# Layer 2's grouped attention: queries and keys of sequences 1 to 7 turned by VectorE blocks and DMA instead of TensorE transposes

## The chip, the cores and the metric

The kernel runs on one core of one Trainium2 chip. The metric is the device time of one execution in microseconds (us). Before the change it is 2081.69 us, the median of three runs (2081.62 to 2082.62). The core has a matrix engine (TensorE, PE in the profile, with its weight loads in the row PEld), a vector engine (VectorE, DVE), an activation engine (ScalarE, ACT), a general engine (GpSimd, POOL), and SyncE (SP), which here issues every DMA. Each engine works through its own list of instructions in order and waits on semaphores for the others. Everything is fp32.

## The reference, cut to what matters

The model has four layers over an input of 8 sequences x 256 tokens x 512 features. Layers 0 and 1 are attention with an MLP, layer 2 is attention alone, and layer 3 is a set of expert MLPs. The change touches layer 2:

```python
def _L2_cond_ref(x, t_emb, W_ada, b_ada, Wq, Wkd, Wku, Wvu, Wo):
    ...                                  # h: layer norm of x, scaled and shifted per sequence
    q = (h @ Wq.T).reshape(B, T, 16, 32).transpose(0, 2, 1, 3)
    c_kv = h @ Wkd.T                     # latent of 128
    k = (c_kv @ Wku.T).reshape(B, T, 4, 32).transpose(0, 2, 1, 3)
    v = (c_kv @ Wvu.T).reshape(B, T, 4, 32).transpose(0, 2, 1, 3)
    q = q * cos + _rotate_half(q) * sin
    k = k * cos + _rotate_half(k) * sin
    ...                                  # each key head serves four query heads
    scores = jnp.einsum('bhtd,bhsd->bhts', q, k_exp) / jnp.sqrt(32)
    scores = jnp.where(mask[None, None], -jnp.inf, scores)
    attn = jax.nn.softmax(scores, axis=-1)
    y = jnp.einsum('bhts,bhsd->bhtd', attn, v_exp)
    return x + y.transpose(0, 2, 1, 3).reshape(B, T, C) @ Wo.T
```

## The kernel before, in words

A token tile is 128 tokens on the 128 partitions, so a sequence is two tiles (`TB`). Products contract over partitions. Projected queries and keys come out with tokens on partitions, but the scores need features on partitions, so both have to be turned by 90 degrees.

**The attention loop.** `attend` (L655) runs the 8 sequences, each with 4 groups of 4 heads. For each group `scored` (L685) issues the score products into four PSUM banks (tag A), and `softmax` (L706) does, head by head, a biased minimum on VectorE (L743) and an exponential with a running sum on ScalarE (L747). Then the weights have to be turned as well. In layer 2, for heads 0 and 1 of each group of the first seven sequences, VectorE transposes 32 x 32 blocks (L752), and five DMAs per group carry the blocks through DRAM (four out in `put`, L545, and one back, L756). For heads 2 and 3 TensorE does three 128 x 128 transposes per head (`turned`, L783), and VectorE or ScalarE copies the result out of PSUM. `weighted` (L808) forms the context, two groups late; `divided` (L830) multiplies by the reciprocal sums.

**The work between the groups.** The rest is dealt into the loop from `self.queue`. `some(us)` (L208) adds a credit and draws generators, each of which yields what its products cost by the author's estimate. It is called three times per group. Two generators matter: `added` (L1310), the output product of the sequence before (eight 128x512 products), and `project2` (L1666), the projection of the next sequence. The projection has the latent (four products of 256 columns), per tile the query product (four of 512 columns), the rotation by `rope` (L649 and L650 on VectorE, then one add on POOL, L1683 for the queries and L1688 for the keys), and the key and value product (L1685). Its input `hT` was normed, turned by VectorE (L534) and sent through DRAM one sequence earlier (`prepare`, `put`, `fetch`; eight DMAs back, L567), and is scaled and shifted at the end of a sequence (L490, L491).

**Queries and keys turned.** `queries_turned` (L1255) makes, per tile, four TensorE transposes of the queries (L1258) into a PSUM bank and one of the keys (L1264), and copies the two banks out, one on VectorE and one on ScalarE (L480, L481, L483, L484). That is ten transposes and four copies per sequence.

**What sets the order.** The program's order is not the order of an engine's list. A scheduler draws instructions at build time, by their priority and by its own estimate of when their inputs are ready, so that work later in the program can be put ahead of an instruction that it expects to wait. `keep_in_program_order` pins chosen instructions. On the chip each list is then worked through strictly in order.

Of the kernel before, what the change touches and what calls it, by code (L numbers as in the profile page):

```python
# [34 lines left out]
P = 128  # L35
# [53 lines left out]
ROUND = 1.5 * 2.0**23  # L89
PI_BELOW = 3.1415925  # L90


# [87 lines left out]
class Program:  # L180
    def __init__(self, ctx, tc, d, out):
        self.ctx, self.tc, self.nc, self.d, self.out = ctx, tc, tc.nc, d, out
        self.n = 0
        self.queue, self.credit = [], 0.0
        self.ready, self.calls = {}, 0
# [22 lines left out]
    def some(self, us):  # L208


        self.credit += us
        self.calls += 1
        while self.credit > 0 and self.queue:
            try:
                did = next(self.queue[0])
            except StopIteration:
                self.queue.pop(0)
                continue
            if did is not None:
                self.credit -= did  # L220
            elif us < 1e6:
                break

    def rest(self):
        self.calls += 100
        self.some(1e9)
        self.credit = 0.0

    def setup(self):
# [39 lines left out]
        self.turns = [self.tc.dram_tile([P, KC * S], F32, name=f"turn{i}") for i in range(3)]  # L271
        self.n_turn = 0
        self.flips = [self.tc.dram_tile([P, 8 * P], F32, name=f"flip{i}") for i in range(4)]
        self.n_flip = 0
# [270 lines left out]
    def put(self, kept, tile):  # L545

        to = kept.rearrange("(c i) (a x) -> a i c x", c=4, a=4)
        for a in range(4):
            self.nc.sync.dma_start(
                to[a], tile[32 * a : 32 * a + 32, :].rearrange("p (c x) -> p c x", c=4)  # L550
            )

    def fetch(self, calls):

        for (name, b), entry in self.ready.items():
            hT, _, kept, _, _ = entry
            if kept is None:
                continue
            entry[2:4] = None, self.calls + calls
            if self.stage(name)[5]:  # L560
                self.nc.sync.dma_start(hT, kept)
                continue
            parts = kept.rearrange("p (a k t j) -> p k t a j", a=4, k=KC, t=TB)
            to = hT.rearrange("p (k t a j) -> p k t a j", k=KC, t=TB, a=4)
            for k in range(KC):
                for t in range(TB):
                    self.nc.sync.dma_start(to[:, k, t], parts[:, k, t])  # L567
# [87 lines left out]
    def attend(self, name, n_groups, hd, project, value, finish, work, key_tiles=(2, 2), biased=None,  # L655
               extra=None, then=None, spare=None, inverse=None, after=None, rooms=None, contexts=None):

# [27 lines left out]
        def scored(b, g):  # L685
# [3 lines left out]
            for j0 in range(0, 4, rows):  # L689
                for q in range(TB):  # L690
                    for j in range(j0, j0 + rows):
                        lhsT, rhs = lhs_rhs[j]
                        keys = rhs(wide[q])
                        if j < self.in_blocks(name, b):

                            keys = keys.rearrange("p (k c i) -> p c k i", c=4, i=32)
                        mm = nc.tensor.matmul(  # L697
# [122 lines left out]
        def divided(b, o, by):  # L820
            for c in range(nch):
                chunks = ctx.setdefault(b, [])
                if b == late:
                    out = spare()[len(chunks)]
                elif contexts is not None:
                    out = contexts[:, b % 2 * 4 + len(chunks), :]
                else:
                    out = self.t([P, S], "ctxT")
# [9 lines left out]
        for i in range(B * n_groups + 1):  # L838
# [59 lines left out]
            else:  # L898
# [5 lines left out]
                while due and due[0][0] <= i:  # L904
                    _, b, g, (pT, by) = due.pop(0)
                    divided(b, weighted(b, g, pT), by)
                    if g == n_groups - 1:
                        if b != late:
                            self.queue.insert(0, outcome(b))
                        got.pop(b)  # L910
# [356 lines left out]
    def project0(self, b, got):  # L1267
# [32 lines left out]
        def scores(g, j):  # L1300
# [3 lines left out]
                lambda q: qT[rows, c, q * P : (q + 1) * P],  # L1304
                lambda n: kT[rows, 0:n],
            )
# [151 lines left out]
    def project1(self, b, got):  # L1458
# [69 lines left out]
        def scores(g, j):  # L1528
            rows = slice(32 * j, 32 * j + 32)
            return (  # L1530
                lambda q: qT[rows, g, q * P : (q + 1) * P],
                lambda n: kT[rows, g, 0:n],
            )
# [132 lines left out]
    def project2(self, b, got):  # L1666
# [3 lines left out]
        qT = self.t([P, KC, S], "qT")  # L1670
        kT, v = self.keys_values(b, ((S,), (TB, P)))
        m = self.bank("C")[:, :S]
        yield from self.product_steps(m, lambda k: w[:, k, 512:640], lambda k: hT[:, k, :])
        cT = self.bank("n")[:, :S]
        nc.scalar.copy(cT, m)
        turn = []
        for t in range(TB):
            cs, sn = self.rope2[:, t, 0, 0, :], [self.rope2[:, t, 1, s, :] for s in range(2)]
            tok = slice(t * P, (t + 1) * P)
            q = self.bank("C")  # L1680
            yield from self.product_steps(q, lambda k: hT[:, k, tok], lambda k: w[:, k, 0:512])
            qr, qb = self.rope(self.bank("qk"), q, cs, sn, 16, 16)
            nc.gpsimd.tensor_tensor(qr, qr, qb, ALU.add)  # L1683
            kv = self.bank("C")[:, :S]
            nc.tensor.matmul(kv, cT[:, tok], w[:, 0, 640:896], start=True, stop=True)  # L1685
            kr, kb = self.rope(self.t([P, P], "kr", 2), kv[:, :P], cs, sn, 4, 16)
            nc.vector.tensor_copy(v[:, t, :], kv[:, P:])
            nc.gpsimd.tensor_tensor(kr, kr, kb, ALU.add)  # L1688
            turn.append((t, qr, kr))
            yield 0.43  # L1690
        for t, qr, kr in turn:
            yield None
            self.queries_turned(t, qT, kT, qr, kr, 1.0 / math.sqrt(32.0))
            yield 0.53

        def scores(g, j):
            rows = slice(32 * j, 32 * j + 32)
            return (
                lambda q: qT[rows, g, q * P : (q + 1) * P],
                lambda n: kT[rows, 0:n],  # L1700
            )
# [4 lines left out]
    def layer2(self):  # L1706
# [10 lines left out]
            inverse=[spare[:, i, :] for i in range(4, 8)],  # L1717
            rooms=self.rooms, contexts=contexts,
        )
# [280 lines left out]
```

## Time and profile before

| what | value |
|---|---|
| median of three runs | 2081.69 us |
| the profiled execution's own time, and its span | 2078.34 us, 2076.6 us |
| PE busy over the span | 2006.0 us (97%) |
| DVE, ACT, POOL busy | 1365.2, 748.1, 334.0 us |
| mean granted TensorE clock | 0.987 |
| layer 2's loop: first score product of sequence 0 to that of sequence 7 | 1668.22 to 1893.51 us |
| mean ns of one: query transpose (L1258), POOL add of the queries (L1683) in the loop | 311, 1333 |

A row of the view by stretches gives the stretch, the busy time of PE, PEld, DVE, ACT and POOL in it with the number of instructions, then the granted TensorE clock (1.00 is full), the mean busy share of the 16 DMA engines and GB/s. In the timeline of an engine a row gives the start, the time to the end of the last of its instructions, the engine, the line, the operation with output and inputs, and in brackets the idle time before it with what ended it. Matmuls overlap, so the time that one costs is the distance from its start to the next start, not its duration.

### The profile page before, as it was taken

How to read it: one execution, taken by the hardware profiler on the slowest of the kernel's cores; microseconds unless marked ns; L12 is line 12 of the kernel's file. 1: busy time of each engine (PE TensorE's matmuls, PEld its weight loads, DVE VectorE, ACT ScalarE, POOL GpSimd, SP SyncE). 2: the span in 40 equal slices, each digit the busy share in tenths (PEclk: the TensorE clock that was granted, in tenths of full speed). 3: DMA queues.
4: the chain of work that ended last, by engine and by line, in shares of the span. 5: the costliest groups of instructions: out<-in, count | busy, mean ns of one | idle time of the engine just before them, and what ended most of it. 6: DMA issues, size and time to landing. Idle time of an engine off the chain costs nothing.

```text
span 2076.6 us, 36333 instructions
## 1 busy us (share of the span) xinstructions
PE 2006.0 (97%) x12818; PEld 1480.9 (71%) x12818; DVE 1365.2 (66%) x4429; ACT 748.1 (36%) x2332; POOL 334.0 (16%) x372
## 2 busy tenths in 40 slices
PE   7999999999999999999999999999999989989999
PEld 4555579999999999954544447999999854445454
DVE  6867766656675555656676766776765678776544
ACT  4333421111111111136565653222222256565644
POOL 1111200000000000054544531000000021101411
PEclk9999999999999999999999999999999989999999
DMA  8543361112130010334555543233211245653411
GB/s 306 166 119 90 102 215 48 65 42 64 61 110 26 17 31 16 96 99 129 131 143 141 141 123 115 89 101 116 87 60 48 67 113 137 158 145 97 126 40 42
DMA packets 223685, 208.91 MB, mean 101 GB/s; under 512 B 83536, under 2 KB 184976, under 8 KB 223120
## 3 DMA queue, kind: packets, MB, share of 16 engines
q1 hardware_dynamic: 223504, 206.59, 34.3%
q8 instruction: 102, 1.67, 0.3%
q14 instruction: 79, 0.65, 0.1%
HBM read 135.46 MB, written 71.07 MB: 99 GB/s over the span
## 4 chain that ended last, share of the span: by engine, by line
PE 78%; DVE 7%; ACT 7%; DMA 4%; issue 2%; POOL 2%; SPq 1%; DVEq 0%; ACTq 0%; POOLq 0%
PE C L1024 29%; PE A L1073 18%; PE C L631 17%; PE A L697 3%; ACT p L747 3%; PE C L808 3%; ACT wbig L747 2%; PE C L783 2%; PE C L1887 2%; PE A L1789 1%; DMA turn<-hT 1%; PE C L1822 1%; DVE st L449 1%; DMA wbig<-in_wgT 1%; DVE n L650 1%
## 5 line engine op out<-in xcount | busy, mean ns | idle before, releaser
L1024 PE MATMUL C<-hT,wbig 128*128 128x128 f32 x3072 | 416.4, 275 | 0.0
L1024 PEld LDWEIGHTS C<-hT,wbig 128*128 128x128 f32 x3072 | 388.8, 192 | 9.0 <-issue 2.4
L631 PE MATMUL C<-wqkv,hT 128*128 128x512 f32 (+1 forms) x768 | 316.6, 553 | 0.9 <-ACT v L1516 0.4
L1073 PE MATMUL A<-wbig,p 128*128 128x256 f32 x1024 | 242.2, 379 | 0.0
L631 PEld LDWEIGHTS C<-wqkv,hT 128*128 128x128 f32 x768 | 134.0, 195 | 122.8 <-issue 108.5
L1073 PEld LDWEIGHTS A<-wbig,p 128*128 128x128 f32 x1024 | 189.7, 190 | 23.1
L1054 DVE TENSOR_TENSOR p<-p,C 128x256 f32<-128x256 f32 x192 | 79.3, 421 | 162.5 <-PE C L1024 160.8
L1044 ACT COPY p<-C 128x128 f32<-128x128 f32 x192 | 51.3, 267 | 370.3 <-PE C L1024 361.8
L1024 PE MATMUL C<-qk,wbig 128*128 128x128 f32 x1152 | 160.0, 275 | 0.0
L1024 PE MATMUL C<-ctxT,wbig 128*128 128x128 f32 x1152 | 160.0, 275 | 0.0
L457 POOL TENSOR_SCALAR r<-mv 128x2 f32<-128x2 f32 (+1 forms) x28 | 7.1, 254 | 929.0 <-DVE mv L450 929.0
L747 ACT ACTIVATE p<-p,low 128x256 f32<-128x256 f32 x256 | 127.3, 501 | 69.9 <-DVE low L743 48.4
L1024 PEld LDWEIGHTS C<-qk,wbig 128*128 128x128 f32 x1152 | 144.1, 192 | 0.0
L1024 PEld LDWEIGHTS C<-ctxT,wbig 128*128 128x128 f32 x1152 | 144.1, 192 | 0.0
L747 ACT ACTIVATE wbig<-wbig,low 128x128 f32<-128x128 f32 (+1 forms) x256 | 113.7, 448 | 78.9 <-DVE low L743 75.9
L1398 ACT ACTIVATE p<-C 128x128 f32<-128x128 f32 x64 | 17.8, 278 | 294.9 <-DVE p L1054 294.9
L1045 DVE TENSOR_TENSOR p<-p,C 128x128 f32<-128x128 f32 x192 | 55.0, 286 | 97.5 <-ACT p L1044 96.4
L631 PE MATMUL C<-wo,ctxT 128*128 128x512 f32 x224 | 103.1, 600 | 1.2 <-DVE ctxT L830 1.2
L1504 POOL TENSOR_TENSOR ss<-ss,neg_half 128x16 f32<-128x16 f32 x32 | 93.8, 2931 | 2.7
L747 ACT ACTIVATE p<-A,low 128x256 f32<-128x256 f32 x128 | 59.3, 486 | 87.0 <-DVE low L727 75.9
L697 PE MATMUL A<-kT,qT 32*128 32x256 f32 (+2 forms) x896 | 85.9, 399 | 1.4 <-ACT p L747 0.6
L697 PEld LDWEIGHTS A<-kT,qT 32*128 32x128 f32 (+1 forms) x896 | 52.4, 191 | 41.9 <-issue 29.0
(268 smaller groups left out, 3507.6 us busy)
## 6 DMA issues: line engine op xcount, KB each, us to landing
flip<-p SPq DMA_DIRECT2D x160, 128.0 KB
p<-flip SPq DMA_DIRECT2D x40, 512.0 KB
turn<-hT SPq DMA_DIRECT2D x120, 128.0 KB
flip<-wbig SPq DMA_DIRECT2D x112, 96.0 KB
wbig<-flip SPq DMA_DIRECT2D x28, 384.0 KB
hT<-turn SPq DMA_DIRECT2D x16, 512.0 KB
kept<-hT SPq DMA_DIRECT2D x16, 512.0 KB
hT<-kept SPq DMA_DIRECT2D x16, 512.0 KB
```

The costliest lines, as they stand in the source:

```text
L631: self.nc.tensor.matmul(out, lhsT(k), rhs(k), start=(k == 0), stop=(k == n - 1))
L697: mm = nc.tensor.matmul(s[j][:, at[q] : at[q] + wide[q]], lhsT(q), keys, start=True, stop=True,)
L747: nc.scalar.activation(out, src, AF.Exp, bias=low[:, q : q + 1], scale=sign, accum_out=tot[:, j, q : q + 1],)
L783: nc.tensor.transpose(m[:, n * P : (n + 1) * P], p[:, at[q] + k * P : at[q] + (k + 1) * P], self.ident,)
L808: mm = nc.tensor.matmul(o[i * hd : (i + 1) * hd, c * S + q0 * P : (c + 1) * S], value(got[b][1], g, j, k), weights(j, mine), start=(k == 0 ...
L1024: nc.tensor.matmul(m[:, c : c + P], w[:, k * P : (k + 1) * P], b[:, k], start=(first and k == 0), stop=(k == steps - 1), skip_group_check= ...
L1044: nc.scalar.copy(g[:, 0, :], m[:, 0:P])
L1045: nc.vector.tensor_tensor(g[:, 0, :], g[:, 0, :], m[:, P : 2 * P], ALU.add)
L1054: nc.vector.tensor_tensor(g[:, 1:3, :], g[:, 0, :].unsqueeze(1).to_broadcast([P, 2, P]), m[:, 2 * P : 4 * P].rearrange("p (i t) -> p i t", ...
L1073: nc.tensor.matmul(acc[at][:, half * S : (half + 1) * S], left, right, start=(p == 0 and half == 0), stop=(p == 3), skip_group_check=True,)
L1504: nc.gpsimd.tensor_tensor(r, r, self.neg_half[:, 0:16], ALU.pow)
L1887: nc.tensor.matmul(m[:, half * S : half * S + S], left[:, r, i, :], right[:, i, :], start=(first and i == 0), stop=(i == 1), skip_group_ch ...
```

## The change: what it does

For sequences 1 to 7, `project2` no longer calls `queries_turned`. POOL's two adds per tile write the rotated queries and keys into a staging tile of 128 x 640 (four query blocks and one key block), in an order that suits 32 x 32 blocks. VectorE transposes the blocks of the staging tile in place, four DMAs put them into DRAM, one DMA fetches the keys into `kT`, one fetches the whole staging tile, and a POOL `tensor_scalar` places the queries in `qT` and scales them. Tile 0's block transpose follows the projection. Tile 1's, the four fetches and the two placings are put on a list `due`, with 2, 3 and 5 more calls of `some` to go; what is still due when the next sequence begins is done then. The block transposes and the placings are pinned. For these sequences the estimates of the projection's products are multiplied by 0.7, so that a given credit draws more of them. `split`, `outputs_between` and the list form of `contexts` change nothing here: `split` is false everywhere. Sequence 0 is turned as before.

```diff
+        turn, late = [], b > 0
+        if late:
+            stages = [self.t([P, 8 * P], "p")[:, : 5 * P] for _ in range(TB)]
+            keeps = [self.pairs[(self.n_pair + t) % 4][:, : 5 * P] for t in range(TB)]
+            self.n_pair += TB
+
+        def dealt(steps):
+            for us in steps:
+                yield us * (0.7 if late else 1.0)
...
-            yield from self.product_steps(q, lambda k: hT[:, k, tok], lambda k: w[:, k, 0:512])
+            yield from dealt(
+                self.product_steps(q, lambda k: hT[:, k, tok], lambda k: w[:, k, 0:512])
+            )
             qr, qb = self.rope(self.bank("qk"), q, cs, sn, 16, 16)
-            nc.gpsimd.tensor_tensor(qr, qr, qb, ALU.add)
+            if late:
+                put = stages[t].rearrange("p (c w i) -> p w c i", c=4, w=5)
+                qr, qb = [x.rearrange("p (k c i) -> p k c i", k=KC, c=4) for x in (qr, qb)]
+                nc.gpsimd.tensor_tensor(put[:, 0:4], qr, qb, ALU.add)
+            else:
+                nc.gpsimd.tensor_tensor(qr, qr, qb, ALU.add)
...
-            yield 0.43
+            yield 0.3
...
+        if late:
+            self.turned_blocks(stages[0], keeps[0])
+
+            def fetched():
+                for t in range(TB):
+                    tok = slice(t * P, (t + 1) * P)
+                    kept = keeps[t].rearrange("p (a w j) -> p a w j", a=4, w=5)
+                    nc.sync.dma_start(kT[:, tok].rearrange("p (a j) -> p a j", a=4), kept[:, :, 4])
+                    nc.sync.dma_start(stages[t], keeps[t])
+
+            def placed():
+                for t in range(TB):
+                    came = stages[t].rearrange("p (a k j) -> p k a j", a=4, k=5)
+                    copy = nc.gpsimd.tensor_scalar(
+                        qT[:, :, t * P : (t + 1) * P].rearrange("p k (a j) -> p k a j", a=4),
+                        came[:, 0:4], scale, None, ALU.mult,
+                    )
+                    self.tc.keep_in_program_order(copy)
+
+            for calls, do in (
+                (2, lambda: self.turned_blocks(stages[1], keeps[1])), (3, fetched), (5, placed)
+            ):
+                self.due.append((self.calls + calls, do))
...
+    def turned_blocks(self, tile, kept):
+        self.tc.keep_in_program_order(self.nc.vector.transpose(tile, tile))
+        self.put(kept, tile)
...
+    def on_time(self):
+        while self.due and self.due[0][0] <= self.calls:
+            self.due.pop(0)[1]()
```

**The order that comes out.** The lists of all engines are the same as before up to the first half of sequence 0's loop, and after layer 2. Between them TensorE's list of one sequence in the middle reads, with S for the scores of a group, T for one of its two sets of three weight transposes, W for its contexts, O for products of the previous sequence's output (the number in brackets says how many), latent, query and kv for the projection, and a prime for what belongs to the next round:

```
before:  S0  T3(prev)  latent+query0  S1  W2(prev)  T0  kv0  query1  T0  query1  W3(prev)
         O(2) S2  T1  O(2)  T1  O(2)  W0  S3  T2  O(2)  T2  kv1  W1
         10 transposes of queries and keys  T3  S0'
after:   S0 (half)  query1(2)  S0 (half)  S1  T0  T0  kv1  W3(prev)  O(4)  S2  T1  O(2)  T1
         O(2)  W0  S3  T2  T2  W1  T3  T3  latent'+query0'  W2  kv0'  query1'(2)  S0'
```

In the changed list the projection that stands ahead of S0' is not that of the sequence whose scores follow, but already that of the one after it. POOL's list has, ahead of the placing of a sequence's tile 0, the two adds of the following projection's tile 0; in the lists of sequences 1, 4 and 5 the placing of tile 1 also stands behind the add of the following projection's query tile 1. VectorE's list has the rotation of that query tile 0, and half of query tile 1, ahead of S0's softmax.

## The prediction

> **What bounds the kernel now.** The shares of the whole span (PE 97%) are set by the MLPs. The lists of all engines differ only inside layer 2's loop, so I read that loop: first the stretches from one sequence's first scores to the next's.
>
> ```profile
> 1735.97:1766.37 30.40, 28.63 (x207) 15.18 (x206) 25.65 (x111) 19.10 (x77) 4.64 (x6) 1.00 0.54 144
> 1766.37:1796.81 30.44, 29.18 (x208) 15.30 (x207) 25.06 (x108) 19.59 (x78) 3.69 (x4) 1.00 0.61 158
> 1796.81:1829.65 32.84, 28.86 (x207) 15.10 (x206) 25.17 (x108) 19.82 (x78) 3.69 (x4) 1.00 0.62 153
> 1829.65:1863.58 33.93, 30.28 (x207) 16.12 (x207) 22.50 (x105) 19.83 (x78) 3.46 (x4) 0.95 0.55 142
> ```
>
> PE is busy some 29 us of a sequence and VectorE some 25: neither has room to wait for the other for long. The loop is fast because PE has projection and output products to do while VectorE and ScalarE work on a group. Next, PE's timeline at a seam between sequences, with the instructions that go:
>
> ```profile
> 1762.60 0.84 PE L808 MATMUL C<-wbig,kT 128*32 128x256 f32 x14
> 1763.91 0.63 PE L1258 MATMUL C<-ident,qk 128*128 128x128 f32 x4 [0.46 <-DVE kr L649]
> 1764.82 0.30 PE L1264 MATMUL C<-ident,kr 128*128 128x128 f32 x1 [0.29 <-ACT wbig L483]
> 1765.38 0.63 PE L1258 MATMUL C<-ident,qk 128*128 128x128 f32 x4 [0.26 <-DVE v L1687]
> 1765.84 0.27 PE L1264 MATMUL C<-ident,kr 128*128 128x128 f32 x1
> 1765.95 0.49 PE L783 MATMUL C<-ident,wbig 128*128 128x128 f32 x3
> 1766.37 1.03 PE L697 MATMUL A<-v,qT 32*128 32x128 f32 x16
> ```
>
> Third, VectorE's and ScalarE's timelines for the distance from start to start, which is what an instruction costs in a chain: four rotation steps take 1.33 us (1780.93 to 1782.26), one group's softmax 2.2 us on VectorE (1785.41 to 1787.62), its block transpose 0.9, one head's exponentials 0.89 on ScalarE (1787.85 to 1788.74), so 3.5 for a group.
>
> ```profile
> 1780.93 0.42 DVE L649 TENSOR_TENSOR qk<-C,row 128x256 f32<-128x256 f32 x1 [0.63 <-PE C L631]
> 1782.26 0.54 DVE L470 TENSOR_SCALAR hT<-x,mv,r 128x512 f32<-128x512 f32 x1
> 1785.41 0.25 DVE L743 CUSTOM_DVE_ANT_0 wbig<-A,row 128x128 f32<-128x128 f32 x1
> 1787.62 0.98 DVE L752 STREAM_TRANSPOSE wbig<-wbig 128x768 f32<-128x768 f32 x1
> 1787.85 0.40 ACT L747 ACTIVATE wbig<-wbig,low 128x128 f32<-128x128 f32 x1
> 1788.74 0.39 ACT L747 ACTIVATE wbig<-wbig,low 128x128 f32<-128x128 f32 x1
> ```
>
> Last, the groups of the loop, for operations that the change adds more of, and the clock after a stall of 1.93 us at 1831.17:
>
> ```profile
> L752 DVE STREAM_TRANSPOSE wbig<-wbig 128x768 f32<-128x768 f32 x28 | 27.4, 977 | 7.5 <-ACT wbig L747 7.4
> L1683 POOL TENSOR_TENSOR qk<-qk,n 128x512 f32<-128x512 f32 x14 | 18.7, 1333 | 95.4 <-DVE n L650 93.5 <-issue 1.9
> L1757 POOL COPY wbig<-x 128x512 f32<-128x512 f32 x4 | 2.3, 615 | 26.3 <-PE C L808 26.3
> ```
>
> ```profile
> 1830.00:1833.00 3.00, 1.17 (x19) 0.59 (x11) 2.29 (x16) 2.25 (x10) 0.00 (x0) 1.00 0.70 157
> 1833.00:1836.00 3.00, 2.90 (x5) 1.72 (x6) 1.94 (x7) 3.00 (x11) 0.00 (x0) 0.51 0.79 214
> ```
>
> **Removed.** Four transposes end 0.63 us after they start and one lasts 0.27, so they stand (0.63 - 0.27)/3 = 0.12 apart; ten are 1.2 us per sequence. The whole stretch that goes, from the end of the contexts (1763.44) to the next transposes (1765.95), is 2.5 us with its waits, 17.5 us over 7 sequences. [...] VectorE and ScalarE lose 0.9 us of copies each.
>
> **Added.** VectorE: two block transposes of 640 columns, 0.90 x 640/768 = 0.75 each, so +0.6 net. POOL: two placings of 128x512 with one input, between 0.62 (the strided copy) and 1.33 (the two-input add); I take 0.62, the nearest in form. SP: twelve DMAs, about 5 us of issue in a sequence whose issues take about 20. Bytes: 2 x (328 + 328 + 66) KB = 1.44 MB on 4.8 MB (158 GB/s x 30.4 us). Way out and back are hidden as long as they land before POOL comes to the placing: tile 1 is transposed at 21.4 on the clock below, four issues take 1.8, the chain of waits shows 3.7 to 4.9 us for such a put and 2.4 back, and SP meets group 3's put (25.4) in between: landed at 29 to 31, needed at 35.8.
>
> **Moved: the order.** This is the large term. I lay the changed lists along one clock, zero at a sequence's S0, with PE's spacing from the timeline: S 0.87, T 0.37, W 0.8, a 512-column product 0.86, a 256-column one 0.43.
>
> S0 in two halves around two query products ends at 2.6. VectorE first does half a rotation (to 2.9), then softmax 0 to 5.1. S1 stands directly behind S0 and needs its banks one by one as VectorE frees them: it ends at 5.6, PE idle 2.1. T0's sets wait for exponentials of heads 2 and 3 (5.8, 6.7): end 7.1, idle 0.8. kv1 and W3 reach 8.35. O's first bank is the one that query tile 1 still holds: VectorE reads the rest of it only after softmax 1 (6.0 to 8.65), the block transpose that waits for ScalarE (9.8) and the last rotation steps: 10.5, PE idle 2.1. O and S2 reach 14.8. VectorE then has key rotation, the new block transpose, a context, the norm and transpose of the next input and a residual add before softmax 2: 16.1 to 18.3. PE does T1, O, T1, O, W0, S3, T2, T2, W1: 22.2. VectorE has softmax 3 from 22.3, behind a reciprocal that waits for exponentials (20.4), the other new block transpose, a residual and a context; ScalarE's exponentials of group 3 end at 26.6. T3 needs them: idle 3.5 and 0.5, end 27.0. Two copies and the scaling of the next input on ScalarE (28.5) hold the second step of latent and query 0 (idle 0.4), which end at 32.5. Now S0' needs the placing, and POOL has the next projection's adds first: rotation 1.34, POOL 1.33 and 0.46, placing 0.62: 36.5, with PE done at 35.6 (idle 0.9). The sum from PE's side: 26 of work and 10.3 idle, 36.3.
>
> Before, five intervals from sequence 1 to 6 took 1863.58 - 1705.97 = 157.6 us; after, 5 x 36.5 = 182.5: **+24.9**. From S3 of sequence 0 (1694.8) to S0 of sequence 1: now 11.2 us. After, T3 ends 2.5 us earlier (1702), then latent, query 0, W, kv and all of query 1 (9.9), rotation, add and placing (3.3): 1715.3, **+9.3**. Sequence 6 has output products behind its groups and no projection at its end: 29 us against 29.9, **-1**. Layer 3: 0.
>
> **Clock.** A half-clock window costs 3 x 0.49 + 3 x 0.08 = 1.7 us (0.51, then 0.92 in the next 3 us); two of the three 1.93 us stalls before latent and query 0 had one (at 1831.2 and 1865.1; after that at 1798.3 the clock stayed at 1.00). [...]
>
> Sum: +40.0. The profiled execution took 2078.34 and would take 2118.3; it lies 3.35 under the median, so 2081.69 + 40.0 = **2122 us**.
>
> **Rivals.** (A) Faster: the stalls don't add up, because the idle parts of one engine cover those of another. For it speak the 2.5 us at each seam, and that the input's DMAs are now issued a group earlier, which removes the three 1.93 us stalls. The order pays when PE's idle time is under 157.6/5 - 26 = 5.5 us per sequence; I count 10.3. At 3 us, 7 x 2.5 = 17.5 go: 2064. Against it: S1 right behind S0, with nothing for PE in between. (B) Half: O's bank or softmax 2 is earlier than I laid it, 3 us a sequence: +15 and +5: 2102. (C) More: on a slower placing (1.33 twice) or with the DMAs landing after 35.8 because SP's list holds puts that wait for VectorE, S0' comes 4 to 6 us later: 2150. (D) The gain and the stalls cancel: 2082.
>
> **Chances.** My forecast 0.64, B 0.13, C 0.10, A 0.10, D 0.03. 0.2% (4 us) is about what a measurement can tell: faster 0.10, same 0.03, slower 0.87. Forecast's own range 2106 to 2138 (placing 0.62 to 1.33, clock none to always). Range 2092 to 2148: it leaves out A, D and half of C.
>
> **What would show it.** Right: S0-to-S0 stretches of 35 to 39 us with PE busy about 27; PE idle before the second scores, before O, and 3 us or more before T3; POOL's placing as releaser of S0; clock under 0.95 in these stretches. Wrong: stretches under 31 us, PE waiting on a DMA for S0, or PE idle only at one place.

## The result: slower by 3.8%, twice the forecast loss

The changed kernel takes 2160.73 us (median of four runs, 2155.72 to 2163.73), the kernel before in the same session 2081.65. The ratio is 1.038, with a 95% interval of 1.036 to 1.040. The sign was forecast, the size was not: +79 us instead of +40, and 2161 lies above the range of 2092 to 2148.

The profiled execution of the changed kernel took 2161.37 us against 2078.34 before, +83.0. By layer 2's own clock the difference splits as follows. The first scores of sequence 0 start 2.55 us later (1670.77 against 1668.22; in the profiles of the experiments below this start lies anywhere between 1665.6 and 1670.5). From there to sequence 1's first scores it is 51.88 us instead of 37.75 (+14.1, forecast +9.3), the five intervals up to sequence 6 are 212.8 instead of 157.6 (+55.2, forecast +24.9), the one from 6 to 7 is 40.70 instead of 29.92 (+10.8, forecast -1), and the rest, from sequence 7's first scores to the end, is equal to within 0.3. That is 82.9 of the 83.0. (The forecast's figures here leave out its +6.8 for the clock.)

First the stretches from first scores to first scores, in the changed kernel (columns as in the same view of the kernel before: length, busy time of PE, PE's weight loads, VectorE, ScalarE, POOL, granted clock, share and GB/s of the DMA engines):

```profile
1722.65:1762.51 39.86, 33.12 (x192) 17.89 (x192) 21.55 (x100) 18.89 (x75) 5.05 (x6) 0.82 0.55 134
1762.51:1803.91 41.40, 35.51 (x197) 18.72 (x197) 25.25 (x109) 18.78 (x75) 7.28 (x9) 0.84 0.57 145
1803.91:1845.21 41.30, 36.49 (x200) 19.08 (x200) 25.34 (x107) 18.98 (x75) 6.27 (x6) 0.83 0.55 140
1845.21:1892.53 47.32, 37.45 (x198) 19.41 (x197) 26.35 (x107) 19.09 (x75) 6.72 (x6) 0.78 0.56 142
1892.53:1935.46 42.93, 29.14 (x187) 16.09 (x186) 22.52 (x99) 19.01 (x75) 5.93 (x5) 0.84 0.54 133
1935.46:1976.16 40.70, 30.69 (x180) 16.40 (x180) 21.12 (x98) 17.53 (x72) 5.18 (x5) 0.75 0.53 146
```

VectorE and ScalarE are no busier than before (25 and 19 us). Of the 55.2 us that the first five stretches are longer, PE's idle time takes 28.4 (41.1 us, 8.2 each, against 2.5 before) and its busy time 26.8 (34.3 each against 29.0), although ten transposes per sequence are gone. The first of the five stretches before, which goes with the four already shown, was:

```profile
1705.97:1735.97 30.00, 28.01 (x202) 14.77 (x202) 26.80 (x113) 18.09 (x74) 5.52 (x8) 0.99 0.52 129
```

In the five of the changed kernel PE is shown busy for 66 us at half clock, against 4 before. The kernel before shows what that does to a product: two of 128x512 take 1.91 us from 1834.09, at a granted clock of 0.50, and 1.02 us from 1802.41, at 1.00. By that an estimate is 31 us of longer busy time, enough for all of it; whether that is a cost of its own is asked below. Next, what is waited for in the loop (us in total, times, longest), and the placings' group of instructions (busy time, mean ns of one, idle time before them):

```profile
PE A L722 <- POOL qT L1761: 31.2, 10, 7.5
...
PE C L808 <- ACT wbig L772: 13.0, 14, 2.3
...
PE A L722 <- DVE low L768: 5.6, 7, 0.8
```

```profile
L1761 POOL TENSOR_SCALAR qT<-p 128x512 f32<-128x512 f32 x14 | 20.9, 1502 | 22.8 <-DMA p<-pair 22.6
```

The largest wait of TensorE is the one for POOL's placing, 31.2 us in the whole loop and 15.6 of the 41.1 in the five stretches. The one ahead of the second scores (L768) and the one ahead of the last transposes (L772), on which the forecast rested, are 5.6 and 13.0.

Where the queries are while TensorE waits is in the timelines of VectorE, SyncE and POOL between sequence 1's first scores (1722.65) and sequence 2's (1762.51). VectorE's block transpose of tile 1:

```profile
1743.49 0.80 DVE L575 STREAM_TRANSPOSE p<-p 128x640 f32<-128x640 f32 x1
```

SyncE (start, time, what it issues):

```profile
1741.62 5.29 SPq L592 DMA_DIRECT2D hT<-turn  x8
1747.00 2.01 SPq L565 DMA_DIRECT2D flip<-wbig  x4
...
1749.77 0.89 SPq L565 DMA_DIRECT2D pair<-p  x2
...
1751.87 0.94 SPq L565 DMA_DIRECT2D pair<-p  x2
...
1753.34 0.57 SPq L1756 DMA_DIRECT2D p<-pair  x1
1754.02 0.37 SPq L565 DMA_DIRECT2D flip<-wbig  x1
...
1757.53 0.50 SPq L1756 DMA_DIRECT2D p<-pair  x1
```

and POOL:

```profile
1759.32 1.27 POOL L1729 TENSOR_TENSOR p<-qk,n 128x512 f32<-128x512 f32 x1 [25.61 <-DVE n L675]
1760.56 0.45 POOL L1738 TENSOR_TENSOR p<-kr,n 128x128 f32<-128x128 f32 x1
1760.98 2.93 POOL L1761 TENSOR_SCALAR qT<-p 128x512 f32<-128x512 f32 x2
```

The tile is ready at 1744.29. Its four puts are issued from 1749.77 to 1752.81, behind eight fetches of the next input and a group's put. Its fetches (keys at 1757.11, blocks at 1757.53) are issued after a gap from 1754.39 in which SyncE waits for the put to land (2.7 us). POOL meanwhile begins the next projection's addition, and both placings follow it: 1763.91, 19.6 us after the transpose. Last, the seam on TensorE:

```profile
1762.51 0.50 PE L722 MATMUL A<-kT,qT 32*128 32x128 f32 x8 [1.65 <-POOL qT L1761]
```

So two chains end close together at this seam: the trip of the blocks, and the next projection with its rotation and additions, behind which POOL's list has the placing. What the placings wait for on POOL, from the view of L1761 (us, times):

```profile
  DMA p<-pair: 22.6, 4
```

These four are the placings of sequences 6 and 7. The other ten start when POOL has ended what stands ahead of them (at the seam shown, the additions), so there the landing is not seen to be the last to end. e1 below shows how close behind it is.

### The profile page after: what moved, and what is told of

Its sections match the earlier page's. It is cut to its first block, busy times and chain, and to the rows that moved or that the text cites. A ratio compares the mean times of both kernels' runs of the same rounds, so it can differ in the third digit from the quotient of the medians.

```text
span 2159.5 us, 36349 instructions
## 1 busy us (share of the span) xinstructions
PE 2044.0 (95%) x12748; PEld 1501.2 (70%) x12748; DVE 1369.1 (63%) x4429; ACT 741.8 (34%) x2318; POOL 353.7 (16%) x386
## 4 chain that ended last, share of the span: by engine, by line
PE 78%; DVE 7%; ACT 5%; DMA 4%; POOL 2%; issue 2%; SPq 1%; DVEq 0%; POOLq 0%; ACTq 0%
PE C L1052 28%; PE C L656 18%; PE A L1101 18%; PE A L722 4%; PE C L833 3%; ACT p L772 3%; PE C L808 2%; PE C L1964 2%; PE A L1866 1%; ACT wbig L772 1%; DMA pair<-p 1%; PE C L1899 1%; DMA flip<-wbig 1%; DVE st L465 1%; DVE n L675 1%
## 5 line engine op out<-in xcount | busy, mean ns | idle before, releaser
L772 ACT ACTIVATE wbig<-wbig,low 128x128 f32<-128x128 f32 (+1 forms) x256 | 112.9, 443 | 143.7 <-DVE low L768 139.0
L772 ACT ACTIVATE p<-p,low 128x256 f32<-128x256 f32 x256 | 126.8, 498 | 70.0 <-DVE low L768 70.0
L722 PE MATMUL A<-kT,qT 32*128 32x256 f32 (+2 forms) x896 | 94.2, 411 | 14.7 <-POOL qT L1761 11.6
L722 PEld LDWEIGHTS A<-kT,qT 32*128 32x128 f32 (+1 forms) x896 | 58.5, 197 | 58.3 <-issue 29.5
L768 DVE CUSTOM_DVE_ANT_0 wbig<-A,row 128x128 f32<-128x128 f32 (+1 forms) x256 | 73.9, 349 | 24.9 <-PE A L722 24.9
```

What stands on the lines that cost most here:

```text
L722: mm = nc.tensor.matmul(s[j][:, at[q] : at[q] + wide[q]], lhsT(q), keys, start=True, stop=True,)
L768: nc.vector.tensor_tensor_reduce(out, src, by, -1.0, BIG, ALU.add, ALU.min, low[:, q : q + 1])
L772: nc.scalar.activation(out, src, AF.Exp, bias=low[:, q : q + 1], scale=sign, accum_out=tot[:, j, q : q + 1],)
```

## The experiments

Four explanations were set against each other. **Trip**: the way of the staged blocks out to DRAM, back and into place ends last, and the next first scores wait for it. **Order**: TensorE's list leaves it too little work behind the first scores and ahead of the last transposes (the forecast's walk), be it through the sooner dealing or through what the blocks do to the list. **Clock**: the half clock that the records show after stalls (126 us in the loop against 27 before) is a cost of its own. **Placing**: POOL's queue, not the DMAs. Differences are to the kernel before in the same session (2077.69 for e1 to e4, 2078.56 for e5 to e8, 2079.71 for e9 to e11, 2079.82 for the last two); the change itself stands at +79.

| run | median us | to before | ratio, 95% interval |
|---|---|---|---|
| e1 placing on ScalarE | 2137.74 | +60 | 1.027 to 1.032 |
| e2 eleven matmuls more per seam | 2157.51 | +80 | 1.035 to 1.041 |
| e3 block DMAs on ScalarE's queue | 2126.37 | +49 | 1.021 to 1.026 |
| e4 dealing as before | 2165.77 | +88 | 1.040 to 1.045 |
| e5 block DMAs on POOL | 2119.99 | +41 | 1.019 to 1.023 |
| e6 e5, placing on ScalarE | 2111.34 | +33 | 1.014 to 1.017 |
| e7 kernel before, dealing alone | 2074.02 | -4.5 | 0.997 to 0.999 |
| e8 sequence 4 alone turned by blocks | 2092.99 | +14 | 1.005 to 1.008 |
| e9 nothing waits for the trip | 2106.64 | +27 | 1.012 to 1.015 |
| e10 tile 1 transposed early | 2121.78 | +42 | 1.018 to 1.022 |
| e11 e6, tile 1 transposed early | 2112.92 | +33 | 1.014 to 1.018 |
| e12 e9, block DMAs on POOL | 2096.15 | +16 | 1.006 to 1.010 |
| e13 e11, dealt sooner still | 2122.76 | +43 | 1.018 to 1.023 |

### Is it the dealing? e4 and e7

```
-                yield us * (0.7 if late else 1.0)
+                yield us
...
-            yield 0.3
+            yield 0.43
```

> The projection is dealt out as before the change (full price of each product, 0.43 after a tile), the turning by blocks stays. If the sooner dealing is what takes TensorE's filling work away from behind the first scores and the last transposes, its idle time falls by 3 to 5 us per sequence: 2120 to 2140. If the round trip of the block turning is the cause, the later projection makes the placing later still: 2165 to 2190. Neither matters: 2155 to 2165.

2165.77: the later projection makes the trip end later, and TensorE's wait for the placing grows from 31.2 to 58.2 us. The other half of the pair is the dealing without the blocks, in the kernel before:

```
+        def dealt(steps):
+            for us in steps:
+                yield us * (0.7 if b > 0 else 1.0)
...
-            yield from self.product_steps(q, lambda k: hT[:, k, tok], lambda k: w[:, k, 0:512])
+            yield from dealt(
+                self.product_steps(q, lambda k: hT[:, k, tok], lambda k: w[:, k, 0:512])
+            )
...
-            yield 0.43
+            yield 0.3
```

> The kernel before, with the sooner dealing alone (0.7 of each product's price for the sequences but the first, 0.3 after a tile); queries and keys are turned by TensorE. If the order on TensorE is a cost of its own (the forecast's idle at the second scores, at the output products and at the last transposes), the loop loses 3 to 5 us per sequence: 2100 to 2115. If the loss of the change is the round trip alone, the dealing by itself costs little: 2072 to 2088.

2074.02, a little faster than the kernel before. One of its stretches (the next is 32.30):

```profile
1731.48:1763.40 31.92, 28.94 (x210) 15.14 (x206) 25.18 (x109) 19.31 (x79) 4.49 (x6) 1.00 0.56 146
```

So sooner dealing by itself costs nothing; the whole loss comes with the turning by blocks. The kernel before with the dealing alone is also the one that beats both kernels.

### Is it the clock? e2

```
             for j0 in range(0, 4, rows):
                 for q in range(TB):
+                    if name == "attention2" and b > 0 and g == 0:
+                        for _ in range((6, 5)[q]):
+                            self.tc.keep_in_program_order(nc.tensor.matmul(
+                                s[0][:, 128 : 384], self.ident,
+                                self.w2[:, 0, :256], start=True, stop=True,
+                            ))
```

> Eleven matmuls of 128x256 that nobody reads (0.43 us each at full clock, 4.7 us in all) stand at each of seven seams, six ahead of the first scores and five between their halves, so that TensorE is busy while it would wait for the placing; their result is overwritten by the scores. If the half clock that follows the stalls is a cost of its own (126 us at half clock against 27 before, some 39 us of TensorE time), the number of half-clock windows falls by a third or more and the time to 2120 to 2145 although 33 us of work are added. If the half clock only fills time that TensorE would have idled, or the other engines set the pace, the time stays or grows: 2160 to 2190.

2157.51: level with the change, 2.5 us under the range for no gain and far from the one for a gain. One stretch of this run, the second:

```profile
1765.85:1807.68 41.83, 38.81 (x218) 21.87 (x218) 25.15 (x109) 19.00 (x75) 7.38 (x9) 0.88 0.58 148
```

The time at half clock in the loop falls from 126 to 82 us, 33 us of matmuls are added, and this stretch stays at 41.8 (41.4 in the change). That does not show that the clock costs nothing. In the list that came out, the six matmuls meant for the seam stand ahead of the last transposes; there they fill the wait for exponentials (13.0 us in the loop before, 0.7 now), while the first scores of sequences 2 and 3 still wait 1.65 and 1.73 us for the placing (in the loop this wait falls from 31.2 to 15.0). And the chain that ended last in this stretch runs along TensorE's list, through the added matmuls and the next projection (start, us, what):

```profile
1766.35 4.04 PE A L720 x10
...
1793.43 2.79 PE A L720 x12
...
1797.42 5.41 PE C L656 x16
```

So the added work was on the path, and what it took came back: from the waits that it filled, and, most likely, from the clock, for the projection's sixteen products take 5.41 us here and, in the changed kernel's chain at the seam shown above, 7.10, of which 3.4 at a granted clock of 0.51:

```profile
1750.64 7.10 PE C L656 x16
```

Gain and loss cancel. How much of the half clock is a cost stays open; an estimate from the 44 us that go is 22 us of TensorE's time at the most.

### Placing or DMAs? e1, e3, e5, e6

```
-                    copy = nc.gpsimd.tensor_scalar(
+                    copy = nc.scalar.activation(
                         qT[:, :, t * P : (t + 1) * P].rearrange("p k (a j) -> p k a j", a=4),
-                        came[:, 0:4], scale, None, ALU.mult,
+                        came[:, 0:4], AF.Copy, scale=scale,
                     )
```

> The two placings of a sequence are made by ScalarE instead of POOL; TensorE's and SyncE's instruction lists stay exactly as in the changed kernel. If POOL's queue is what the first scores wait for (two placings of 1.49 us behind the next projection's additions of 1.27 us), TensorE's 31 us of waiting for the placing fall to 10 to 15 and some half-clock windows with them: 2120 to 2140 us. If the landing of the block DMAs is what comes last, the placing only changes its engine: 2150 to 2162. If the idle at the first scores is covered elsewhere anyway (VectorE or ScalarE is the bound), also no change: 2155 to 2165.

2137.74, and TensorE's and SyncE's lists are unchanged (VectorE's but for two neighbours), so this is the cleanest of the comparisons. ScalarE does a placing in 0.63 us and no longer behind the next additions. What it now waits for is the landing (50.0 us in 12 times):

```profile
ACT qT L1761 <- DMA p<-pair: 50.0, 12, 7.6
```

A quarter of the loss was the placing, and close behind it comes the landing.

This run also shows what is left where the queries come in time. Two of its stretches, and all that TensorE waits for in them:

```profile
1755.76:1794.63 38.87, 33.16 (x198) 17.28 (x197) 25.26 (x109) 19.84 (x77) 4.33 (x7) 0.91 0.60 155
1794.63:1834.96 40.33, 34.56 (x202) 18.09 (x201) 25.25 (x107) 19.51 (x77) 3.65 (x5) 0.92 0.57 144
```

```profile
PE C L808 <- ACT wbig L772: 4.8, 6, 2.3
PE C L656 <- DVE n L675: 2.9, 2, 2.1
PE A L722 <- DVE low L768: 1.7, 2, 0.8
PE C L833 <- DMA wbig<-flip: 1.0, 1, 1.0
PE C L656 <- PE C L808: 0.8, 2, 0.4
```

No scores wait for their queries here, and still the two stretches take 79.2 us, where two average ones before took 63. What TensorE waits for are the forecast's places (last transposes, output products, second scores), with 13.7 us at half clock. So these stretches are 7 to 9 us longer than before even with the queries in place. The likeliest cause is the changed list on TensorE, in which the next projection stands ahead of the first scores, with the half clock that the records show there; DMAs show in these waits with 1.0 us only. By e7 it is not the dealing: there the projection stands behind the first scores again. No run here changes that order and nothing else.

Two runs move them to another queue, e3 as shown, e5 with `gpsimd` in place of `scalar`:

```
     def turned_blocks(self, tile, kept):
...
-        self.put(kept, tile)
+        to = kept.rearrange("(c i) (a x) -> a i c x", c=4, a=4)
+        for a in range(4):
+            self.nc.scalar.dma_start(
+                to[a], tile[32 * a : 32 * a + 32, :].rearrange("p (c x) -> p c x", c=4)
+            )
...
-                    nc.sync.dma_start(kT[:, tok].rearrange("p (a j) -> p a j", a=4), kept[:, :, 4])
-                    nc.sync.dma_start(stages[t], keeps[t])
+                    nc.scalar.dma_start(kT[:, tok].rearrange("p (a j) -> p a j", a=4), kept[:, :, 4])
+                    nc.scalar.dma_start(stages[t], keeps[t])
```

> The block DMAs of queries and keys (eight out, four back per sequence) are issued by ScalarE's queue instead of SyncE's. If SyncE's list is what makes them late (tile 1 is transposed 22 us after the sequence's first scores, its first put is issued 5.5 us later and its fetch 13 us later), the fetch comes 4 to 6 us sooner, the waits for the placing shrink: 2125 to 2145. If POOL's queue or the order on TensorE is the cause: 2150 to 2165. If ScalarE's exponentials are held up by these DMAs' waits: 2165 to 2200.

> The block DMAs of queries and keys are issued by POOL, which has nothing else to do between a tile's additions and its placing; the placing stays on POOL and now stands ahead of the next projection's additions in five of the seven sequences. If the round trip is long because the DMAs wait in SyncE's list (18 us from the end of tile 1's block transpose to the next first scores, of which the bare trip is about 8), the next first scores come at 30 to 33 us instead of 40 to 41: 2085 to 2115. If the issue on POOL is slow or the clock is a cost of its own, less is gained: 2115 to 2140. If the order of the groups on TensorE (the forecast's walk) sets the pace, the period stays at 36 us or more and the time at 2120 to 2160.

2126.37 and 2119.99: out of SyncE's list the blocks are worth 30 to 38 us, nearly half of the loss. In both runs TensorE's order is another one too, so this is not the queue alone. The trip theory's own number for e5, first scores every 30 to 33 us, was not reached: from sequence 1 to 6 they stand 35.9 apart, just short of the 36 that were to speak for TensorE's order. e6 puts both together:

> As the run with the block DMAs on POOL, and the placing on ScalarE besides (0.63 us instead of 1.49). If the round trip sets the period, each seam gains at most the difference of two placings, 1.7 us, so 5 to 12 us less than the run before it. If TensorE or VectorE set the period once the DMAs are early, it is equal within 4 us. If ScalarE then waits for the landing with exponentials behind it, it is slower by 5 or more.

2111.34, 9 us less, as the trip theory had it. Here the trip can be seen without a queue. POOL's timeline, tile 1 of sequence 3 (VectorE ends its transpose at 1770.64):

```profile
1771.33 2.26 POOL L578 DMA_DIRECT2D pair<-p  x4
1776.28 0.79 POOL L1759 DMA_DIRECT2D v<-pair  x1 [2.70 <-DMA pair<-p]
1777.07 0.56 POOL L1760 DMA_DIRECT2D p<-pair  x1
```

ScalarE's placing, and the scores that wait for it on TensorE:

```profile
1781.41 0.63 ACT L1765 ACTIVATE qT<-p 128x512 f32<-128x512 f32 x1 [3.99 <-DMA p<-pair]
```

```profile
1782.10 1.24 PE L726 MATMUL A<-v,qT 32*128 32x256 f32 x8 [1.97 <-ACT qT L1765]
```

From 1770.64 to 1782.04 are 11.4 us, of which the two landings are 2.7 and 3.8. In the kernel before, the whole stretch with the ten transposes and their waits was 2.5 us.

### One seam: e8

```
-        turn, late = [], b > 0
+        turn, late = [], b == 4
```

> Sequence 4 alone is turned by blocks and dealt sooner, the others as before the change. If each seam costs by itself, a seventh of 83 us: 2088 to 2094. If the cost comes from the chain that runs from one sequence's first scores through its projection to the next one's (each late seam delays the next projection), one seam between two early ones is partly made up: 2078 to 2086. If it only moves the order for the worse around it: over 2096.

2092.99, +14.4, somewhat more than a seventh of 79: each seam costs by itself, and the next ones don't make it up. TensorE waits 6.3 us for the placing at this one.

### Taking the wait away: e9 and e12

```
             def fetched():
                 for t in range(TB):
-                    tok = slice(t * P, (t + 1) * P)
-                    kept = keeps[t].rearrange("p (a w j) -> p a w j", a=4, w=5)
-                    nc.sync.dma_start(kT[:, tok].rearrange("p (a j) -> p a j", a=4), kept[:, :, 4])
                     nc.sync.dma_start(stages[t], keeps[t])
...
                     self.tc.keep_in_program_order(copy)
+                    tok = slice(t * P, (t + 1) * P)
+                    nc.gpsimd.tensor_copy(
+                        kT[:, tok].rearrange("p (a j) -> p a j", a=4), came[:, 4]
+                    )
...
-                (2, lambda: self.turned_blocks(stages[1], keeps[1])), (3, fetched), (5, placed)
+                (2, lambda: self.turned_blocks(stages[1], keeps[1])), (5, placed), (5, fetched)
```

> All the work of the changed kernel stays, but the placing (and a copy of the keys, two more instructions of 128x128 on POOL per sequence) reads the staged blocks before they go out and back, so nothing waits for the round trip; the fetch of the keys is left out. Left out of the computation: the exchange of 32-row blocks between partitions, so that the scores are of other numbers. If the wait for the round trip is the loss, the first scores come 31 to 33 us after the last ones: 2075 to 2100. If the dealing, the clock or VectorE's added transposes are, it stays at 2135 or more; the traffic alone (the writes and the fetches of the staged blocks stay) would show as what is left over the kernel before.

2106.64: 52 of the 79 us go with the trip. That is outside both expectations, and nearer to the trip's. It is not the wait alone: with nothing to wait for, TensorE's list has the first scores in one piece again and the next projection behind them, so this run takes away the wait and the changed order together. What is left shows on TensorE behind the first scores of sequence 3, and on VectorE:

```profile
1777.30 2.90 PE L656 MATMUL C<-hT,wqkv 128*128 128x256 f32 x6 [4.52 <-issue]
```

```profile
1776.79 0.74 DVE L506 TENSOR_SCALAR hT<-hT,mod 128x256 f32<-128x256 f32 x2
```

The next input is scaled only at 1776.79, and its eight fetches were issued from 1767.81, behind four of the block DMAs (1764.69 to 1767.22). In SyncE's list the block DMAs make the next input late even where nobody waits for the blocks. e12 takes them out of that list:

> As the run in which nothing waits for the round trip (the exchange of 32-row blocks is again left out), but with the block DMAs issued by POOL instead of SyncE. That run still stood 27 us over the kernel before, with TensorE idle for 4.5 us behind the first scores for the next input, whose eight fetches were issued 1 us ahead of the first scores; with TensorE's transposes and the same dealing they are issued 3.9 us ahead. If the block DMAs in SyncE's list hold those fetches back, SyncE is now free of them: 2070 to 2085. If VectorE's order (two softmaxes ahead of the scaling of the input) is at fault by itself, or the DMA traffic, it stays at 2098 to 2112.

2096.15. The stall is down to 1.44 us, and 10.5 of the 27 us are gone:

```profile
1778.31 1.19 PE L660 MATMUL C<-hT,wqkv 128*128 128x256 f32 x2 [1.44 <-issue]
```

The other 16 us were not separated. At this seam TensorE waits for POOL's placings and key copies, at least 14.4 us in the whole loop (6.1 + 5.0 + 3.3), and e12 carries two such copies per sequence that the change has not.

### Can the trip be hidden? e10, e11, e13

```
-            for calls, do in (
-                (2, lambda: self.turned_blocks(stages[1], keeps[1])), (3, fetched), (5, placed)
-            ):
+            self.turned_blocks(stages[1], keeps[1])
+            for calls, do in ((1, fetched), (3, placed)):
                 self.due.append((self.calls + calls, do))
```

> Tile 1's block transpose is no longer put off by two calls but made right behind tile 0's; the fetch comes at the first call after and the placing at the third; SyncE, POOL and all counts as in the changed kernel. If the late start of the trip is half of the loss (the transpose stands some 10 us behind tile 1's additions), the first scores come 6 to 10 us sooner: 2095 to 2125. If SyncE's list decides when the blocks go out, whatever the transposes do: 2145 to 2160. If VectorE's transposes ahead of a softmax hold up exponentials: over 2160.

> Early block transposes, the block DMAs on POOL and the placing on ScalarE together. If the first scores then find their queries in place, TensorE has no wait at the seam and the loop is that of the kernel before less ten transposes: 2065 to 2080, level with the kernel before or better. If the trip still ends last: 2085 to 2105. If VectorE or ScalarE suffer from the early transposes and placings: about as the run without early transposes, 2105 to 2115.

2121.78 and 2112.92. Beginning earlier is worth 37 us with the DMAs on SyncE, as the first expectation of e10 had it. Added to e6 it is worth nothing: in e11 the trip still ends last, and TensorE waits 32.3 us for the placing. Tile 1's additions end only 21 to 25 us after the first scores. The projection dealt out sooner (0.4 and 0.2) takes that away:

> Early block transposes, block DMAs on POOL, placing on ScalarE, and the projection dealt out sooner still (0.4 of the price, 0.2 after a tile). The trip then begins when tile 1's additions end, now some 23 us after the first scores, and takes about 13. If the additions end 4 to 6 us sooner the trip fits into the period and the seam's wait of about 4 us goes: 2075 to 2095. If TensorE then lacks products to do behind the later groups, the wait only moves to the last transposes: 2100 to 2120.

```profile
1772.12 1.15 PE L726 MATMUL A<-kT,qT 32*128 32x128 f32 x16
1776.69 2.06 PE L812 MATMUL C<-ident,wbig 128*128 128x128 f32 x6 [3.43 <-ACT wbig L776]
...
1784.42 0.67 PE L660 MATMUL C<-hT,wqkv 128*128 128x256 f32 x2 [1.67 <-DVE hT L506]
```

The wait for the queries is gone (0.7 us in the whole loop), and the time is 2122.76, worse than e11. TensorE now waits 20.5 us for exponentials ahead of transposes and 11.4 for the next input: the products that used to fill these places have been done already. Hiding the trip and filling the last groups draw on the same work.

## Why the prediction was right in sign and wrong in size

**The step that failed** is the one that reads "Way out and back are hidden as long as they land before POOL comes to the placing: ... landed at 29 to 31, needed at 35.8". On the same clock (zero at 1722.65) the transpose of tile 1 ended at 21.6, as forecast (21.4). Then nothing was as forecast: first put at 27.1, last at 30.2, fetch at 34.9, placings from 38.3 to 41.3, next first scores at 39.9. I had added up issue and landing times and let SyncE meet one group's put; its list also held eight fetches of the next input (5.3 us), and the fetch of the blocks waits at the head of that list until the put has landed (2.7 us). From e1, where a placing starts 3.0 to 5.0 us after its fetch is issued, the blocks landed at about 38 to 40 (an estimate), not 29 to 31. The runs bear out that the trip costs: DMAs out of that list 30 to 38 us, an earlier start 37, a faster placing 19, no trip at all 52. These overlap, all but the placing also change TensorE's order, and they don't add up to the 79. At the seam on this clock the trip was not alone: POOL's additions of the next projection, which the forecast did count, ended at 38.3 and released the placings.

**The placing** was taken as 0.62 us, bounded by 1.33. It is 1.50, above the bound. The row chosen as nearest in form was a copy. Moved to ScalarE, where it takes 0.63, and out of POOL's list, it brings 19 us, 2.7 at each of seven seams.

**The walk** had its places of idle time right and their total nearly so: forecast 10.3 us per steady interval, measured 8.2, of which 3.1 are waits for the placing. In the stretch from 1762.51 the second scores waited 0.85 (forecast 2.1), the output products 0.71 (2.1), the last transposes 1.9 and 0.3 (3.5 and 0.5), the first scores 1.7 (0.9), and up to 5.7 at later seams. By e7 and e4 the sooner dealing is not what costs. Without any wait for queries e1 still has stretches that are 7 to 9 us longer, most likely by this walk and its clock.

**The clock** was the term of the sum that was too small by most: the walk had 26 us of TensorE's work in an interval, and it took 34.3. No run shows the +6.8 that the sum has for the clock in the whole loop (1.7 us after four of six long stalls, the author's estimate). Measured in its place are 126 us at half clock in the loop against 27, and TensorE is busy in these for 77 us more; an estimate from this is 39 us of longer busy time. How much of that the result would lose at full clock stays open: part of it would turn into waits for the queries, and e2 does not separate the two.

**From sequence 6 to 7** I forecast -1, with "no projection at its end". Sequence 7's queries make their trip in that very interval, and the first scores of sequence 7 wait twice, 3.1 and 2.7 us: +10.8. **The first interval** has +14.1 instead of +9.3: POOL does both of sequence 2's additions and a normalization ahead of sequence 1's placings, which start at 1721.09 though TensorE has been waiting since 1715.2.

**Removed and added work** were nearly right (block transpose 0.81 for 0.75), and small. **The rivals**: C named much of what happened, a slower placing and DMAs that are late because of SyncE's list, and got 0.10 and 2150. Its own 4 to 6 us at each of seven seams make 2150 to 2164, which takes in the 2161. A, B and D fell. The range of 2106 to 2138 is also wider than the two causes that it names give (2115 to 2130, with 1.7 us for the clock in none to all six of those stalls). The right sign was no mere luck, for stalls at the places that the walk named did come; but half of the size came from terms that the sum had at nothing or too small.

## What to carry to other kernels

Replacing a 1.2 us operation on a busy engine by a chain through DRAM takes work off that engine but puts a latency between producer and consumer: 11 us in the run without a queue in the way, 20 in the change, behind SyncE's list and POOL's additions. Count that chain from the last producer to the first consumer of the next round, queue by queue, before counting what is saved. In the change a fetch waited 2.7 us at the head of SyncE's list for the put to land, and what stood behind it was issued only then (from 1757.53); and with the block DMAs ahead of the next input's fetches TensorE stalled for that input by 4.52 us (e9), with them on POOL by 1.44 (e12). A consumer that has to wait also moves in the list: here the next projection went ahead of the first scores, and stretches stayed 7 to 9 us longer even where the wait was gone. And work added to a stall is a test only with its own trace: where the added work stands on the chain that ended last, an unchanged time means that gain and loss cancel.

## What the runs showed of the hardware that I had not expected

The clock fell after shorter gaps than the 1.93 us that I had read from the kernel before, and for longer than the 3.4 us that it was down after two of those. In the changed kernel, with gaps of 1.65 us at 1760.9 and 0.85 us at 1765.6 (windows, columns as above):

```profile
1760.00:1767.80 7.80, 5.30 (x34) 2.71 (x33) 3.07 (x19) 1.83 (x9) 3.92 (x4) 1.00 0.48 145
1767.80:1779.00 11.20, 10.48 (x40) 5.62 (x38) 9.34 (x36) 6.13 (x27) 1.68 (x2) 0.54 0.51 126
```

TensorE is shown busy for 10.5 of the 11.2 us of the second window, in which the granted clock was 0.54. (The second scores are shown busy for 2.88 of the 2.90 us from 1766.4, while VectorE's minimums ahead of them end one by one up to 1767.9; whether TensorE waited in between, the records do not show.) Every half-clock period of both kernels' loops, five before and sixteen in the change, is 3.4, 6.8, 10.2, 13.6 or 17.1 us long, to the resolution of windows of 0.25 us. The length of a gap alone does not tell what follows: gaps of 1.65 and 0.85 us came ahead of 10.2 us at half clock here, and in the kernel before, the one of 1.93 us at 1798.3 was followed by a clock of 1.00 up to 1805. What sets off a half-clock period no run here shows.

The same strided scaling of 128x512 takes a median of 1.49 us on POOL (the change) and 0.63 on ScalarE (e6). Issued by POOL, four puts take 2.3 us to issue (e6), and puts and fetches of the blocks land a median of 4.2 us after issue (e5).
